# A two-layer GCN and an attention mix on one core: another preparation of degrees, and gather buffers by the chunk

## The chip, the cores and the metric

The kernel runs on one core of a Trainium2 chip. The metric is the device time of one execution in microseconds (us); less is better. PE is TensorE, with PEld its weight loads, DVE is VectorE, ACT is ScalarE, POOL is GpSimd and SP is SyncE, which here only issues DMAs. ACT and POOL issue DMAs too.

## The reference

There are N = 12,500 nodes with D = 256 features and E = 200,000 edges, whose `dst` is sorted. Cut to what matters:

```python
def _gcn_conv(x, W, b, src, dst, n):
    h = x @ W
    ones = jnp.ones(src.shape[0], dtype=x.dtype)
    deg = jax.ops.segment_sum(ones, dst, num_segments=n)
    dinv = jnp.where(deg > 0, jax.lax.rsqrt(deg), 0.0)
    norm = dinv[src] * dinv[dst]
    msgs = h[src] * norm[:, None]
    out = jax.ops.segment_sum(msgs, dst, num_segments=n)
    return out + b

# with self loops appended to src and dst
h = jnp.maximum(_layernorm(x, axis=-1), 0.0)
h = h @ W_pre + b_pre
h = relu(_gcn_conv(h, W1, b1, src, dst, n))
h = relu(_gcn_conv(h, W2, b2, src, dst, n))
x = x + (h @ W_post + b_post)
# a second layer on x: layer norm, relu, x @ weight in 4 heads of 64, a softmax over heads
# of leaky_relu(alpha_l + alpha_r) for the first n edges, a mix of the heads, added to x
```

## The kernel before

The edges are cut into chunks of 14 tiles of 128 edges (`J` = 14, `CE` = 1792): `NCH` = 112 chunks. The nodes form `NT` = 98 tiles of 128, handled in `NG` = 14 groups of `G` = 7. The kernel has four stages.

**Preparation (0 to 161.8 us).** `load_edges` (L536, L538, on SP) brings `dst` and `src` into SBUF as one row per chunk: 111 whole rows in one DMA and the short last one in another. POOL fetches `a_raw`, the first `dst` of every tile, with 30 small DMAs (L561 to L572). `load_x` (L585, on SP) brings node groups into 11 `fxt` buffers. POOL writes constants: `sel`, `iota_r`, `iota_a`, `slide`, `zeros`. DVE casts the list (`fdst_f`, L621) and forms `near` (`dst` less a multiple of 16 per tile) and `to_f` (`dst` less the chunk's first); PE turns these and `src` (`turned`), which gives `near_t`, `to_t` and the gather indices `src_t`.

The degrees are a histogram by products, in four parts of 28 chunks (`NPT`, `CP`). `count_block` compares `near_t` with `iota_r` on DVE (`hot_r`, L699) for four of a chunk's tile positions at a time and sums over edges on PE (`tiles`). `place` adds each part's tiles into the long count: ACT copies `tiles_b`, DVE makes `hot_n` (L722) from the tiles' first ends `a_bf`, PE multiplies (`count`, L728), ACT copies (`counted`), and PE spreads the counts over partitions (`fdegs`, L747). Between blocks, `stats(s)` takes the layer norm's mean and variance of group s (L754, L756). `norms(k)` (L763 on) makes 1/sqrt(degree) and the scales of part k's node tiles, then scales each of its groups (`relu(x * sc + nb)` on ACT at L782; in the last part every second tile on DVE at L778 and L780), writes it to `ftable1` with dinv in a further column (SP, L784), and issues the load of a later group into the freed buffer. `w_of` gives the node tiles that each part completes.

After that come checks of each chunk's range (`lo`, `hi`, `keeps`; they set `bad_row`, by which a general path would be run), the offset of each chunk's window (`offs`), the base of each chunk spread over partitions (`wide`, `base_b`), and the weights of the later products: `fwb`, `fwo` and `fwg`, whose last columns are DVE products with the attention vectors (`far`, `fprod`, L885, L886).

**Pass 1 (161.8 to 2140.4 us) and pass 2 (2140.4 to 4138.2 us).** `convolve` runs over all tiles of all chunks. For each tile POOL gathers 128 rows of the table by an indirect DMA into one of 64 `fgot` buffers (L1043), and PE multiplies them with a one-hot matrix of the destinations (`fhot`, made by DVE for a whole chunk at its predecessor's third tile) and accumulates a chunk in `facc` (L1048). At a chunk's end `close` copies the sums by ACT and puts later steps on a list ordered by tile number: 8 tiles on, PE turns the sums (`fturn`); 13 tiles on, DVE adds them into a sliding window `buf`, and for every node tile that is then complete `finish1` or `finish2` has its steps put on the list, 6, 10 or more tiles on. In pass 1 these are the product with `wf` (`fpo`) and the relu `fo`, which is written to `ftable2`. Pass 2 gathers from `ftable2`; its finish does the second layer's products.

**Mix (4138.2 to 4279.9 us).** POOL gathers the attention terms (`fal`, L1235), and DVE does the softmax and the mix.

Each engine's instructions run in the order in which the program issues them (`manual_schedule`); semaphores for the dependencies between engines are put in by the framework. A tile from a pool with `bufs=n` waits until the n-th tile before it in that name is no longer read.

Of the kernel before, what the change touches and what calls it, by code (L numbers as in the profile page):

```python
# [8 lines left out]
F32 = mybir.dt.float32  # L9
BF16 = mybir.dt.bfloat16  # L10
# [403 lines left out]
def fast_path(  # L414
# [69 lines left out]
    nc.vector.memset(eps, EPS)  # L484

# [7 lines left out]
    row_i = const.tile([P, AC], I32, name="row_i")  # L493
    lane = const.tile([P, 1], F32, name="lane")
    nc.gpsimd.iota(lane, pattern=[[0, 1]], base=0, channel_multiplier=1,
                   allow_small_or_imprecise_dtypes=True)

    def load_w(w, name):
        t = const.tile([P, KC, w.shape[1]], F32, name=name)
        nc.scalar.dma_start(t, w.rearrange("(k p) n -> p k n", p=P))  # L500
        return t
# [5 lines left out]
    with tc.tile_pool(name="fprep", bufs=1) as prep:  # L507
# [3 lines left out]

        LB = 16
        R = 2 * LB
        NL = 2 * LAG + P
        NPT = 4
        CP = NCH // NPT
        L = 7
        Q = CP // L
        I = J * Q
        JB = 4  # L520
        NA = NT * P // LB
        AW = (CP * M + 2 * LAG + P) // LB + 2
        assert NPT * CP == NCH and Q * L == CP and M * CP % LB == 0 and AW % 2 == 0
        a_of = [max(M * CP * k - LAG, 0) // LB for k in range(NPT)]

        w_of = [0] + [((CP * M * (k + 1) - LAG) // P) // G * G for k in range(NPT - 1)] + [NT]
# [4 lines left out]
        def load_edges(e, pad, name):  # L531
            t = prep.tile([NCH, CE], I32, name=name)

            if last < CE:
                nc.vector.memset(t[:, last:], pad)
            nc.sync.dma_start(t[:NCH - 1, :],  # L536
                              e[:(NCH - 1) * CE].rearrange("(c e) -> c e", e=CE))
            nc.sync.dma_start(t[NCH - 1:NCH, :last], e[None, (NCH - 1) * CE:])  # L538
            return t

        dst_r = load_edges(dst, NOWHERE, "fdst_r")
        src_r = load_edges(src, 0, "fsrc_r")
# [8 lines left out]


        a_raw = prep.tile([I, NPT, L], I32, name="a_raw")
        nc.gpsimd.memset(a_raw, NOWHERE)
        for k in range(NPT):
            whole = min(E // CE - k * CP, CP)
            d = dst[k * CP * CE:(k * CP + whole // L * L) * CE].rearrange(
                "(q l j e) -> j q l e", l=L, j=J, e=P)
            a = a_raw[:, k, :].rearrange("(j q) l -> j q l", q=Q)
            for q in range(whole // L):  # L560
                nc.gpsimd.dma_start(a[:, q, :], d[:, q, :, 0])  # L561
            for l in range(whole % L):
                c = k * CP + whole // L * L + l
                nc.gpsimd.dma_start(
                    a[:, whole // L, l:l + 1],
                    dst[c * CE:(c + 1) * CE].rearrange("(j e) -> j e", e=P)[:, 0:1])
        if last < CE:
            j = -(-last // P)
            e = (NCH - 1) * CE
            a = a_raw[:, NPT - 1, L - 1:L].rearrange("(j q) l -> j q l", q=Q)[:, Q - 1]  # L570
            for n in range(j):
                nc.gpsimd.dma_start(a[n:n + 1], dst[None, e + n * P:e + n * P + 1])  # L572
# [19 lines left out]
        for g in range(XB):  # L592
            load_x(g)

# [3 lines left out]
        for r0, base, keep in ((0, 0, [-1, LB - 1]), (R, LB, [1, -LB])):  # L600
# [5 lines left out]
        iota_r = prep.tile([P, R, JB * CP], BF16, name="iota_r")  # L606
        nc.gpsimd.iota(iota_r, pattern=[[1, R], [0, JB * CP]], base=0, channel_multiplier=0,
                       allow_small_or_imprecise_dtypes=True)
        iota_a = prep.tile([I, L, AW], BF16, name="iota_a")
        nc.gpsimd.iota(iota_a, pattern=[[0, L], [1, AW]], base=0, channel_multiplier=0,  # L610
                       allow_small_or_imprecise_dtypes=True)

        slide = prep.tile([P, 2 * I - 1], BF16, name="slide")
        nc.gpsimd.memset(slide, 0.0)
        nc.gpsimd.memset(slide[:, I - 1:I], 1.0)
        zeros = prep.tile([1, 512], BF16, name="zeros")
        nc.gpsimd.memset(zeros, 0.0)


        dst_f = prep.tile([NCH, CE], F32, name="fdst_f")  # L620
        nc.vector.tensor_copy(dst_f, dst_r)  # L621
# [7 lines left out]
                                dst_f.rearrange("c (j e) -> c j e", e=P),  # L629
                                low[:, :, None].to_broadcast([NCH, J, P]), ALU.subtract)  # L630
        base = prep.tile([NCH, 1], F32, name="base")
        nc.vector.tensor_copy(base, dst_f[:, 0:1])
        to_f = dst_f
        nc.vector.tensor_scalar(to_f, dst_f, base, None, op0=ALU.subtract)
        src_f = prep.tile([NCH, CE], F32, name="fsrc_f")
        nc.scalar.activation(src_f, src_r, AF.Copy)
# [8 lines left out]

        with tc.tile_pool(name="wpsum", bufs=2, space=PSUM) as psum:
            wpt = prep.tile([P, KC, D], F32, name="wpt")
            for k in range(KC):
                pt = psum.tile([P, D], F32, name="fw")
                for i in range(KC):  # L650
                    nc.tensor.transpose(pt[:, i * P:(i + 1) * P], wp[:, i, k * P:(k + 1) * P],
                                        ident)
                nc.vector.tensor_copy(wpt[:, k, :], pt)
            for i in range(KC):
# [4 lines left out]
                nc.vector.tensor_copy(wf[:, i, :], pw)  # L659
# [4 lines left out]
            nc.vector.tensor_copy(bb[:1, :], pw[:1, :])  # L664

        with tc.tile_pool(name="fpsum", bufs=2, space=PSUM) as psum, \
# [20 lines left out]
            turned(near, near_t, nc.vector.tensor_copy)  # L687
            turned(to_f, to_t.rearrange("p c j -> p j c"), by_act)
            turned(src_f, src_t.rearrange("p c j -> p j c"), by_act)
            a_int = prep.tile([I, NPT, L], I32, name="a_int")  # L690
            a_bf = prep.tile([I, NPT, L], BF16, name="a_bf")
# [3 lines left out]
            def count_block(k, j0):  # L695
                n = min(JB, J - j0)
                hot = prep.tile([P, R, JB, CP], BF16, name="hot_r", bufs=2)
                near = near_t[:, None, j0:j0 + n, k * CP:(k + 1) * CP]
                nc.vector.tensor_tensor(  # L699
                    hot[:, :, :n, :], near.to_broadcast([P, R, n, CP]),  # L700
                    iota_r[:, :, :n * CP].rearrange("p r (j c) -> p r j c", c=CP), ALU.is_equal)
                if j0 == 0:
                    parts[k] = cpsum.tile([I, R, L], F32, name="tiles", bufs=2)
                for j in range(n):
                    for q in range(Q):
                        i = (j0 + j) * Q + q
                        nc.tensor.matmul(parts[k], slide[:, I - 1 - i:2 * I - 1 - i],
                                         hot[:, :, j, q * L:(q + 1) * L], start=(i == 0),
                                         stop=(i == I - 1))

            def place(k):

                if k == 0:
                    nc.vector.tensor_scalar(a_int, a_raw, LB.bit_length() - 1, None,
                                            op0=ALU.arith_shift_right)
                    for m in range(NPT):
                        nc.vector.tensor_scalar(a_bf[:, m, :], a_int[:, m, :], -float(a_of[m]),
                                                None, op0=ALU.add)
                tiles = prep.tile([I, R, L], BF16, name="tiles_b", bufs=2)
                nc.scalar.activation(tiles, parts[k], AF.Copy)  # L720
                hot = prep.tile([I, L, AW], BF16, name="hot_n", bufs=2)
                nc.vector.tensor_tensor(hot, a_bf[:, k, :, None].to_broadcast([I, L, AW]),  # L722
                                        iota_a, ALU.is_equal)
                a0, a1 = a_of[k], min(a_of[k] + AW, NA)
# [34 lines left out]
            def norms(k):  # L759
# [11 lines left out]
                for g in range(w0 // G, w1 // G):  # L771
                    t = xs[g]
                    nc.vector.tensor_copy(t[:, :, D], dinv[:, g * G:(g + 1) * G])
                    for i in range(G):
                        w = g * G + i
                        h = t[:, i, :D]
                        if k == NPT - 1 and i % 2:
                            nc.vector.tensor_scalar(h, h, sc[:, w:w + 1], nb[:, w:w + 1],  # L778
                                                    op0=ALU.mult, op1=ALU.add)
                            nc.vector.tensor_scalar(h, h, 0.0, None, op0=ALU.max)  # L780
                        else:
                            nc.scalar.activation(h, h, AF.Relu, bias=nb[:, w:w + 1],  # L782
                                                 scale=sc[:, w:w + 1])
                    nc.sync.dma_start(  # L784
                        table1[g * G * P:(g + 1) * G * P, :].rearrange("(c p) d -> p c d", p=P), t)
                    if g + XB < NG:
                        load_x(g + XB)
                nc.vector.reciprocal(dinv2[:, w0:w1], deg[:, w0:w1])

            blocks = [(k, j0) for k in range(NPT) for j0 in range(0, J, JB)]  # L790
            for s, (k, j0) in enumerate(blocks):
                count_block(k, j0)
                if s < NG:
                    stats(s)
# [529 lines left out]
```

## Time and profile before

| | us |
|---|---|
| median of 3 runs | 4279.28 (4278.62 to 4281.58) |
| the profiled execution's own time | 4281.77 |
| its span in the profile | 4279.9 |
| of it: preparation, pass 1, pass 2, mix | 161.8, 1978.6, 1997.8, 141.7 |
| granted TensorE clock, mean | 0.80 |

The profile is of one execution. Its stages are cut at the first gather of each pass and at the first gather of `fal`. A busy share is an average over stages with different limits; idle time ahead of an instruction is put down to the semaphore event that came last before it, and "issue" means that the profile shows nothing that the engine waited for.

### The profile page before, as it was taken

Reading aid. Unit: us, or ns where it says so; the run is one execution under the profiler, and the core shown is the slowest. Engines: PE = TensorE matmul, PEld = TensorE weight load, DVE = VectorE, ACT = ScalarE, POOL = GpSimd, SP = SyncE. Lnnn points to the kernel's source line nnn. Section 1 sums busy time; section 2 is a strip of 40 time slices with the busy share of each in tenths; the row PEclk is TensorE's granted clock in tenths of the full one; section 3 lists DMA queues with packets and bytes.
Section 4 is the critical chain, followed back from the end, with each engine's and each line's share of the span. In section 5 each row is a group of like instructions: output and inputs, shape, how many; then the busy total and the mean of one; then the engine's idle time right before and its main releaser. Section 6 shows DMA issues by size and latency. Waiting matters only on the chain. (4 is left out here: it accounts for less than half of the span.)

```text
span 4279.9 us, 35030 instructions
## 1 busy us (share of the span) xinstructions
PE 3309.1 (77%) x10832; PEld 2027.9 (47%) x10832; DVE 1116.9 (26%) x2279; ACT 407.6 (10%) x1054; POOL 3115.8 (73%) x3297
## 2 busy tenths in 40 slices
PE   5587887878777888778768778777788778887773
PEld 3344444444444444444345555555555545555552
DVE  7422222222222222222122222222222222222238
ACT  3200000000000000000001111111111111111122
POOL 2377777777777777777677777777777777777766
PEclk7677777777777777877878888988888898888886
DMA  5544444444444444444344444444444444444456
GB/s 181 151 118 119 120 121 119 119 119 121 118 119 119 123 119 119 118 121 119 107 142 134 127 124 126 126 123 124 123 127 123 123 123 127 123 123 124 127 155 188
DMA packets 301080, 543.65 MB, mean 127 GB/s; under 512 B 84053, under 2 KB 199508, under 8 KB 300884
## 3 DMA queue, kind: packets, MB, share of 16 engines
q0 software_dynamic: 154480, 414.28, 37.1%
q1 hardware_dynamic: 114958, 111.19, 8.3%
q10 hardware_dynamic: 31446, 15.83, 1.3%
q8 instruction: 90, 1.47, 0.1%
q14 instruction: 106, 0.87, 0.1%
HBM read 488.01 MB, written 52.93 MB: 126 GB/s over the span
## 5 line engine op out<-in xcount | busy, mean ns | idle before, releaser
L1043 POOL DMA_INDIRECT fgot<-ftable,fsrc_t x3126 | 2982.8, 954 | 1026.7 <-issue 474.2
L1048 PE MATMUL facc<-fgot,fhot 128*128 128x257 f32 (+1 forms) x6252 | 2385.5, 500 | 774.3 <-DMA fgot<-ftable,fsrc_t 738.5
L1048 PEld LDWEIGHTS facc<-fgot,fhot 128*128 128x128 f32 x6252 | 1233.1, 230 | 1784.6 <-DMA fgot<-ftable,fsrc_t 1451.2
L997 DVE TENSOR_TENSOR buf<-buf,fturn 128x256 f32 x224 | 94.5, 422 | 1707.0 <-PE fturn L941 1675.0
L974 DVE TENSOR_TENSOR fhot<-iota_p,to_t 128x1792 f32<-128x1792 f32 x224 | 448.3, 2003 | 0.1
L1129 DVE SCALAR_TENSOR_TENSOR fx<-fpo,fdinv,fxb 128x256 f32<-128x256 f32 x97 | 46.9, 484 | 1311.2 <-PE fpo L1125 1311.2
L981 ACT ACTIVATE fsums<-facc 128x257 f32<-128x257 f32 (+1 forms) x224 | 86.4, 386 | 1352.9 <-PE facc L1048 1352.8
L1077 PE MATMUL fpo<-wf,buf 128*128 128x256 f32 x388 | 162.3, 565 | 0.4 <-DVE buf L997 0.4
L1112 PE MATMUL fpz<-buf,fwb 128*128 128x128 f32 x776 | 147.2, 319 | 0.0
L1077 PEld LDWEIGHTS fpo<-wf,buf 128*128 128x128 f32 x388 | 118.3, 305 | 30.8 <-DVE buf L997 0.7
L1235 POOL DMA_INDIRECT fal<-table_l,fsrc_t x98 | 94.9, 968 | 50.6 <-issue 27.1
L1112 PEld LDWEIGHTS fpz<-buf,fwb 128*128 128x128 f32 x776 | 121.2, 220 | 14.9 <-issue 3.6
L1082 ACT ACTIVATE fo<-fpo,fdinv 128x256 f32<-128x256 f32 x97 | 46.0, 474 | 807.5 <-PE fpo L1078 807.5
L941 PE MATMUL fturn<-fident,self 128*128 128x128 f32 x396 | 89.5, 314 | 34.7 <-DMA self<-ftable 30.0
L1124 PE MATMUL fpo<-fwo,fz 128*128 128x256 f32 x388 | 114.8, 422 | 0.0
L1114 PE MATMUL fpz<-rm,fb2r 1*128 1x128 f32 x388 | 104.3, 352 | 0.0
L941 PE MATMUL fturn<-fident,fsums 128*128 128x128 f32 x448 | 101.7, 315 | 0.5 <-ACT fsums L981 0.5
L1226 PE MATMUL fends<-rows,hot_t 128*128 128x260 f32 x196 | 67.7, 519 | 39.7 <-ACT fxg L1228 39.4
L1013 DVE COPY buf<-buf 128x640 f32<-128x640 f32 x194 | 97.5, 502 | 3.3
L941 PEld LDWEIGHTS fturn<-fident,fsums 128*128 128x128 f32 x448 | 74.3, 166 | 35.9 <-issue 13.1
L1078 PE MATMUL fpo<-bb,fins 2*128 2x256 f32 x194 | 87.3, 537 | 0.0
L941 PEld LDWEIGHTS fturn<-fident,self 128*128 128x128 f32 x396 | 59.9, 167 | 42.9 <-issue 31.6
(198 smaller groups left out, 1602.0 us busy)
## 6 DMA issues: line engine op xcount, KB each, us to landing
fgot<-ftable,fsrc_t POOLq DMA_INDIRECT x3126, 2.8
ftable<-fxt SPq DMA_DIRECT2D x14, 910.0 KB
self<-ftable SPq DMA_DIRECT2D x97, 130.0 KB
ftable<-fo ACTq DMA_DIRECT2D x98, 128.0 KB
kept_x<-fx SPq DMA_DIRECT2D x98, 128.0 KB
fxr<-kept_x SPq DMA_DIRECT2D x14, 896.0 KB
self<-ftable SPq DMA_DIRECT2D x97, 128.0 KB
fxb<-in_x_dram SPq DMA_DIRECT2D x97, 128.0 KB
```

Of the source, the lines that this page charges most:

```text
L941: nc.tensor.transpose(v["pt"][:, i * KC + k, :], rows[:, k * P:(k + 1) * P], ident)
L974: nc.vector.tensor_tensor(h[:, :n, :], iota_p[:, None, :].to_broadcast([P, n, P]), to_t[:, c, :n, None].to_broadcast([P, n, P]), ALU.is_equal)
L997: nc.vector.tensor_add(b, b, v["pt"][:, :KC, :])
L1013: nc.vector.tensor_copy(nxt[:, :, :BW - P], buf[:, :, P:])
L1043: nc.gpsimd.indirect_dma_start(out=got, out_offset=None, in_=table[:], in_offset=bass.IndirectOffsetOnAxis(ap=src_t[:, c, j:j + 1], axis=0))
L1048: nc.tensor.matmul(acc, hots[c][:, j, :], got[:, :width], start=(j == 0), stop=(j == nj[c] - 1))
L1077: nc.tensor.matmul(po, buf[:, k, :P], wf[:, k, :], start=(k == 0), stop=False)
L1078: nc.tensor.matmul(po, fs, bb, start=False, stop=True)
L1112: nc.tensor.matmul(pz[:, m, :], wb[:, k, m * P:(m + 1) * P], buf[:, k, :P], start=(k == 0), stop=False)
L1114: nc.tensor.matmul(pz[:, m, :], b2r[:, m * P:(m + 1) * P], v["rm"], start=False, stop=True)
L1124: nc.tensor.matmul(po, v["z"][:, m, :], wo[:, m, :], start=(m == 0), stop=False)
L1235: nc.gpsimd.indirect_dma_start(out=al[:, i, :], out_offset=None, in_=table_l[:], in_offset=bass.IndirectOffsetOnAxis(ap=src_t[:, c, j:j + ...
```

## The change

1. `load_edges` issues the 111 whole rows as two DMAs of 96 and 15 rows. The `src` list is issued behind the first two loads of x.
2. The 30 DMAs of `a_raw` and the shift and subtraction on it go. In their place a 0/1 tensor `perm`, made on POOL, is reduced in two ways (`by_kq`, `by_kl`); POOL multiplies `low` with the one (`low_q`), PE multiplies that with the other, and ACT scales the product into `a_bf`.
3. POOL's constants are made in another order: `zeros`, `slide` and `iota_r` first, `sel` last.
4. DVE works on the integer list itself (no `fdst_f`). The copies of `wpt`, `wf`, `bb` and `near_t` move from DVE to ACT. An activation `warm` at the start loads the Sqrt table. `src` is cast and turned after the second block.
5. The degrees are counted in five parts of 28, 28, 28, 21 and 7 chunks (`c_of`), with as many tile positions per block as fit (`JB`). `stats(0)` runs before the first block, and then each block is followed by the next group's `stats`. `norms` only lists its groups in `to_scale`; one of them is scaled after each block, and those left over at the end. The copy of dinv into its column moves from DVE to POOL. `dinv2` is taken once, at the end.
6. The small operations for `offs` move up, most of them to POOL. The check of the chunks' ranges is now made from `to_t` (`check_chunks`), and the loads of the late weights and the products with `far` become `load_late`; both are called in pass 1 after the first `fo`.
7. `fgot` is allocated once per chunk as a tile of 14 gathers, with 4 buffers, in place of 64 buffers of one gather.

The diff, cut to its core:

```diff
-        NPT = 4
-        CP = NCH // NPT
+        c_of = [0, 28, 56, 84, 105, NCH]
+        NPT = len(c_of) - 1
+        CP = [c_of[k + 1] - c_of[k] for k in range(NPT)]
...
-        JB = 4
+        BLOCK = 4 * max(CP)
+        JB = [min(BLOCK // n, J) for n in CP]
...
-            nc.sync.dma_start(t[:NCH - 1, :],
-                              e[:(NCH - 1) * CE].rearrange("(c e) -> c e", e=CE))
+            some = (NCH - 1) // 16 * 16
+            for c0, c1 in ((0, some), (some, NCH - 1)):
+                nc.sync.dma_start(t[c0:c1, :],
+                                  e[c0 * CE:c1 * CE].rearrange("(c e) -> c e", e=CE))
...
-        src_r = load_edges(src, 0, "fsrc_r")
...
-        a_raw = prep.tile([I, NPT, L], I32, name="a_raw")
-        nc.gpsimd.memset(a_raw, NOWHERE)
...
         for g in range(XB):
             load_x(g)
+            if g == 1:
+                src_r = load_edges(src, 0, "fsrc_r")
...
+        perm = prep.tile([NCH, NPT, max(Q), L], F32, name="perm")
+        nc.gpsimd.memset(perm, 0.0)
+        for k in range(NPT):
+            p = perm[:, k, :Q[k], :]
+            nc.gpsimd.affine_select(out=p, in_=p, compare_op=ALU.not_equal, fill=1.0,
+                                    base=-c_of[k], pattern=[[-L, Q[k]], [-1, L]],
+                                    channel_multiplier=1)
...
-        dst_f = prep.tile([NCH, CE], F32, name="fdst_f")
-        nc.vector.tensor_copy(dst_f, dst_r)
...
+        for k, q in enumerate(Q):
+            nc.gpsimd.tensor_mul(low_q[k], low[:, :, None].to_broadcast([NCH, J, q]),
+                                 by_kq[:, k, None, :q].to_broadcast([NCH, J, q]))
...
+        nc.gpsimd.tensor_copy(mean_i, mean)
+        nc.vector.tensor_scalar(mean_i, mean_i, ~(P - 1), None, op0=ALU.bitwise_and)
...
-            turned(near, near_t, nc.vector.tensor_copy)
+            turned(near, near_t, by_act)
+            a_bf = prep.tile([I, NPT, L], BF16, name="a_bf")
+            pa = psum.tile([I, NPT, L], F32, name="ft")
+            for k, q in enumerate(Q):
+                nc.tensor.matmul(pa[:J * q, k, :], low_q[k].rearrange("c j q -> c (j q)"),
+                                 by_kl[:, k, :], start=True, stop=True)
+                nc.scalar.activation(a_bf[:J * q, k, :], pa[:J * q, k, :], AF.Copy,
+                                     scale=1.0 / LB, bias=-float(a_of[k]))
...
+            stats(0)
+            blocks = [(k, j0) for k in range(NPT) for j0 in range(0, J, JB[k])]
             for s, (k, j0) in enumerate(blocks):
                 count_block(k, j0)
-                if s < NG:
-                    stats(s)
+                if s + 1 < NG:
+                    stats(s + 1)
...
+                if s == 1:
+                    turn_src()
+                if to_scale:
+                    scale(k == NPT - 1)
             norms(NPT - 1)
+            while to_scale:
+                scale(True)
+            nc.vector.reciprocal(dinv2, deg)
...
-            got = ep.tile([P, stride], F32, name="fgot", bufs=ahead)
+            if j == 0:
+                gots = ep.tile([P, J, stride], F32, name="fgot", bufs=ahead)
+            got = gots[:, j, :]
...
             nc.scalar.dma_start(table2[w * P:(w + 1) * P, :], o)
+            if w == 0:
+                load_late(work)
+                check_chunks(work, psum)
...
-        convolve(ep, table1, D1, D + 1, 64, True, psum, lambda w: prepare1(work, w),
+        convolve(ep, table1, D1, D + 1, 4, True, psum, lambda w: prepare1(work, w),
...
-        convolve(ep, table2, D, D, 64, False, psum, lambda w: prepare2(work, w),
+        convolve(ep, table2, D, D, 4, False, psum, lambda w: prepare2(work, w),
```

## The prediction, made before the changed kernel ran

> **What bounds the kernel now.** I read the page's totals first, then the table of busy time by stage, then what GpSimd (POOL) waits for.
>
> ```profile
> span 4279.9 us, 35030 instructions
> PE 3309.1 (77%) x10832; PEld 2027.9 (47%) x10832; DVE 1116.9 (26%) x2279; ACT 407.6 (10%) x1054; POOL 3115.8 (73%) x3297
> ...
> L1043 POOL DMA_INDIRECT fgot<-ftable,fsrc_t x3126 | 2982.8, 954 | 1026.7 <-issue 474.2
> ```
>
> ```profile
> 0.00:161.80 161.80, 75.23 (x395) 58.81 (x395) 107.72 (x343) 61.09 (x129) 31.27 (x66) 0.69 0.59 182
> 161.80:2140.40 1978.60, 1585.26 (x4343) 863.83 (x4341) 421.31 (x831) 89.85 (x210) 1491.09 (x1564) 0.76 0.44 119
> 2140.40:4138.20 1997.80, 1583.25 (x5906) 1056.10 (x5907) 482.34 (x919) 218.49 (x604) 1498.63 (x1570) 0.85 0.47 125
> 4138.20:4279.90 141.70, 65.31 (x192) 49.19 (x190) 105.56 (x186) 38.16 (x112) 94.86 (x98) 0.72 0.69 210
> ```
>
> The columns are length, then busy us (instructions) of PE, PEld, DVE, ACT and POOL, then clock, DMA share and GB/s. Both passes are rows of gathers on POOL: 1,563 of them at 1.251 us each (0.947 busy, 0.305 before the next) make 1,955 of pass 1's 1,979 us. PE is busy 80% of a pass, but is only a follower: a gather's matmul ends 3.4 to 9.2 us after that gather starts, 28.0 once, as pass 2 begins.
>
> ```profile
> POOL fgot L1043 <- issue: 474.2, 1519, 11.6
> POOL fgot L1043 <- PE facc L1048: 382.3, 1255, 0.3
> POOL fgot L1043 <- DVE sbuf L957: 63.2, 1, 63.2
> ```
>
> 382.3 us is put down to PE, yet no wait among the 1,255 is over 0.3 us, the gap that gathers with no such wait have too. The first 64 gathers take fresh buffers and never wait for PE. Here are 63 of them beside 63 later ones, which all do:
>
> ```profile
> L1043 POOL DMA_INDIRECT fgot<-ftable,fsrc_t x63 | 60.0, 952 | 82.1 <-DVE sbuf L957 63.2 <-issue 18.9
> ...
> L1043 POOL DMA_INDIRECT fgot<-ftable,fsrc_t x63 | 60.4, 959 | 19.2 <-issue 11.3 <-PE facc L1048 6.1 <-PE fsum L943 0.6
> ```
>
> 18.9 us of gaps without, 19.2 with. So the passes go by POOL's own rate, and what can move is the 161.8 us before the first gather. There VectorE (DVE) is the chain:
>
> ```profile
> 17.25 1.09 DVE L621 CAST fdst_f<-fdst_r 112x1792 f32<-112x1792 int32 x1 [14.81 <-DMA fdst_r<-in_dst_dram]
> 37.67 1.37 DVE L682 CAST near_t<-ft 128x448 bf16<-128x448 f32 x2 [9.74 <-PE ft L680]
> 40.23 2.02 DVE L699 TENSOR_TENSOR hot_r<-near_t,iota_r 128x3584 bf16<-128x3584 bf16 x1
> 134.24 0.19 DVE L763 TENSOR_SCALAR fdeg<-fdegs 128x28 f32<-128x28 f32 x1 [15.03 <-PE fdegs L747]
> 143.81 1.96 DVE L804 TENSOR_REDUCE flo<-fdst_f 112x1 f32<-112x1792 f32 x1
> 157.51 0.42 DVE L885 TENSOR_TENSOR fprod<-fwg,far 128x256 f32<-128x256 f32 x1 [3.14 <-DMA self<-ftable]
> 161.81 1.04 POOL L1043 DMA_INDIRECT fgot<-ftable,fsrc_t  x1 [63.23 <-DVE sbuf L957]
> ```
>
> It waits for the edge list until 17.25; for POOL's constants (PE's first matmul needs `zeros`, ready at 35.6 behind 18 us of `a_raw` DMAs) until 37.67; counts from 40.23 with hardly a break to 119.2; waits 15 us for the last fourth of the degrees; scales four groups (8.2 us); checks chunks from 143.81 to 152.57; and makes `fwg` last. The last four writes of `ftable1`, which share the queues with weight loads, end at about 152.
>
> **Part 1, a start 21 us earlier.** The trace shows the 111 rows of `dst` moving three at a time, 37 rows per DMA engine, 3.8 to 16.5. As 96, 15 and 1 rows they can use more engines: six rows each of about 0.3 to 0.55 us. I take a landing at 8. Bounds: 6.5 (uncontended) and 17.25 (unspread, as now). [...]
>
> DVE drops the 1.09 cast; low, `near`, base and `to_f` (0.17+0.17+2.02+0.15+1.15) with two reductions end about 12.8. It then meets `mean_i`, which waits for POOL. POOL's list without `a_raw`: 1.7 + memsets 0.70 + zeros 0.51 + slide 0.31 + `iota_r` 3.29 = 6.5; perm (a memset, five selects of 0.1 to 0.3) 7.4; `iota_a` 1.54, 8.9; sel 5.6, 14.5; five `low_q` products, which no row shows: between 0.1 (small memset) and 1.08 (select on 1,024 elements), I take 0.2, nearest in size, 15.5; mean 16.1. Then `stats(0)`, 2.8 us, to 19.0, and the first `hot_r` at 19.0 in place of 40.23. Its other input, `near_t`, moves to ACT: the table load of 1.28 us, now at the head of ACT's queue, delays the weight loads' issue by as much, the weight chain (PE products, copies of about 0.4 on ACT) ends near 13.4, and four copies of 0.87 end by 17.6, inside that wait. The product for the tiles' ends (five PE-ACT rounds of about 0.8) and the `to_t` copies end at 25.3 on ACT; nothing needs the ends before the first `hot_n`. On SP the `src` load now stands behind x 0 and x 1: at 2.6 to 3.3 us a load, as the x loads take now, it lands near 17, x 2 near 20 and x 10 near 45, each ahead of its `stats` (one per 4.6 us); `src` is first read after block 1, about 28.
>
> **Part 2, counting to the last degrees.** DVE's sum stays: `hot_r` 27 us, 13 remaining `stats` at 2.77 = 36, `hot_n` 6.8, four `norms` about 4.9: 74.6 us, so 19.0 → 93.6. What follows is the short last part (7 chunks) on PE and ACT: third part's degrees (count 1.4, copy 0.7, eight matmuls 3.6) at 98.9, last block 101.1, its count, copy and degrees 107.0. Its `norms` end at 108.6, against 135.4 now. Interleaved scaling of g0 to g8, one group a block, lies on ACT under the blocks; their writes and the loads of x 11 to 13 on SP run one a block, 4.6 us apart, each 2.8 us of transfer. If that cover fails, the later `stats` are late by one transfer. The copy of `dinv` moves to POOL (0.17 on DVE), which has nothing else then but memsets waiting for those writes.
>
> **Part 3, the last groups and the exit.** Now four groups are scaled last, then five, 2.03 each: 108.6 + 10.2 = 118.7. The first is ready to write at 110.6 and five writes at 2.8 us (8.4 us for three in the trace where no weight shared the queue) drain at about 125.2, landing at 126. DVE's remainder (dinv2, `offs`, degrees, `wide`, `root_t`) ends at 122.6, under the drain. Chunk checks (8.8) and `fwg` (3.25 plus 3.14 waiting) have left this path, and weight loads too. With the 1 us that POOL takes over semaphores now, the first gather is at 127: 161.8 − 127 = **35 us earlier**.
>
> **Part 4, inside pass 1.** `load_late` and `check_chunks` follow the first `fo`, at about gather 50: some eight issues on ACT (0.5 each), a stall of 6 to 8 us for the second `far` buffer, 15 us of DVE work and waits, three transposes on PE. Behind DVE's wait stand the next `fhot` (2.0 us) and so PE's matmuls; POOL feels it only when a buffer is not free. Cost 0. Without that cover, up to 15 us.
>
> **Part 5, one tile per chunk.** 2,998 waits of POOL for PE become 216, each chunk's first gather waiting for the matmul 43 gathers before it, 43 × 1.251 = 53.8 us of slack against 9.2 (28.0 once). By the two rows of 63 gathers the dropped waits are worth 0.3 us in 63, or nothing; bounds 0 to 2,782 × 5 ns = 14 us of gain. I take 0. About 104 gathers, some 47 in each pass, last 1.0 to 1.7 us and cost 23 us in all; they come at the same places of a chunk whether the gather carries no, one or two waits, so I leave them. The stretch between the passes (11.6) and the ending stay.
>
> **Sum.** 4281.77 (profiled execution, 1.87 outside its span) − 35 = 4246.8. It stands 2.5 above the median, so 4279.3 − 35 = **4244.3**, say 4245.
>
> **Rivals.** *Less from preparation* (0.16): `dst` unspread, so the change does not do what it says (−5.5, since POOL's list hides the rest), `low_q` at its upper end (−4.4), a drain at 3.5 us a write (−3.5). Together the gain is 21.6: 4258. For: ACT carries more, and no row shows most of POOL's small products. Against: the waits of 14.81 and 9.74 have visible causes that go.
>
> *Faster passes* (0.05): if part of the 0.305 gap is the handling of a wait, 20 ns each is 56 us, 4189. The two rows of 63 speak against. [...]
>
> *Slower* (0.06): releasing by the chunk makes POOL wait. Place: each chunk's first gather; it decides once PE runs over 53.8 us behind. At 0.3 us for each of 216 waits it costs 65, net +30: 4309; the break-even is 0.16 us a wait. Against: PE has 20% of a pass free, so even the stall of part 4 is worked off within some four chunks. For: a buffer comes free only when its whole chunk is multiplied, and part 4 lands on PE while the queue is full.
>
> *Preparation gains under 9* (0.03): a stall in the x loads behind writes on SP, 4272 to 4279.
>
> **Chances and range.** Forecast 0.70, a gain of 25 to 42 (25: the bounds of part 1 and a drain that is 3 us longer; 42: the drain keeps pace, so that the last write ends 3.8 after 118.7, and POOL's list is 3 us shorter). The measurement tells about 0.2%, 8.6 us, from no change. Faster: 0.70 + 0.16 + 0.05 = 0.91; same 0.03; slower 0.06. The range takes in the forecast's bounds (4237 to 4254), most of the lesser gain (to 4262), and 5 us at the lower end for part 5's bound in the gaps: 4232 to 4262.
>
> **What would show it.** First `hot_r` at about 19; no wait over 2 us on DVE before the third part's degrees; the last degrees at 107; first gather at 127; gathers at 1.251, gap 0.305, and no POOL wait for PE above 0.3. Wrong if the gap shrinks in every gather, or first gathers of chunks wait, or the first gather comes after 140.

## The result, and the profile after

The changed kernel takes 4245.18 us (median of 4, 4243.32 to 4246.28) against 4279.75 for the kernel before: a ratio of 0.9918, 95% interval 0.9901 to 0.9936. That is 34.6 us less; 35 were forecast. Its page and its table by stage (the columns are those explained in the prediction):

```profile
span 4243.1 us, 32312 instructions
PE 3275.7 (77%) x10867; PEld 2000.0 (47%) x10867; DVE 1116.3 (26%) x2257; ACT 409.1 (10%) x1066; POOL 3102.3 (73%) x3304
...
L1077 POOL DMA_INDIRECT fgot<-ftable,fsrc_t x3126 | 2978.4, 953 | 985.1 <-issue 954.1
```

```profile
0.00:126.50 126.50, 74.47 (x421) 58.82 (x421) 98.24 (x298) 62.77 (x141) 22.62 (x74) 0.68 0.71 222
126.50:2106.20 1979.70, 1568.72 (x4350) 852.22 (x4350) 430.29 (x854) 89.83 (x210) 1489.19 (x1563) 0.77 0.43 119
2106.20:4101.30 1995.10, 1566.38 (x5906) 1039.26 (x5907) 482.50 (x919) 218.52 (x604) 1495.76 (x1570) 0.86 0.47 125
4101.30:4243.10 141.80, 66.14 (x192) 49.72 (x190) 105.32 (x186) 38.03 (x112) 94.75 (x98) 0.72 0.69 209
```

Preparation is 35.3 us shorter, and the other three stages moved by +1.1, −2.7 and +0.1 us. The page's instruction count fell by 2,718 (POOL alone has 2,783 semaphore waits fewer), and the gathers did not notice: 953 ns each, 954 before. What POOL waits for changed its name and not its amount:

```profile
POOL fgot L1077 <- issue: 954.1, 3024, 18.8
POOL fgot L1077 <- PE facc L1082: 25.0, 82, 0.3
```

The 382.3 us that were put down to PE are now "issue"; the gap of 0.3 us stays in front of every gather. The steps of preparation, on DVE, POOL and ACT:

```profile
9.13 0.82 DVE L614 TENSOR_SCALAR low_i<-fdst_r 112x14 int32<-112x14 int32 x1 [6.69 <-DMA fdst_r<-in_dst_dram]
10.19 2.81 DVE L619 TENSOR_TENSOR near_f<-fdst_r,low 112x1792 f32<-112x1792 int32 x1
18.94 0.15 DVE L651 TENSOR_SCALAR mean_i<-mean_i 112x1 int32<-112x1 int32 x1 [4.03 <-POOL mean_i L650]
21.78 2.00 DVE L734 TENSOR_TENSOR hot_r<-near_t,iota_r 128x3584 bf16<-128x3584 bf16 x1
99.15 0.18 DVE L794 TENSOR_SCALAR fdeg<-fdegs 128x21 f32<-128x21 f32 x1 [2.37 <-PE fdegs L778]
103.36 0.29 DVE L798 RECIPROCAL fdinv<-froot 128x21 f32<-128x21 f32 x1 [3.83 <-ACT froot L796]
106.75 0.17 DVE L794 TENSOR_SCALAR fdeg<-fdegs 128x7 f32<-128x7 f32 x1 [0.72 <-PE fdegs L778]
```

```profile
11.19 2.77 POOL L609 TENSOR_SCALAR_AFFINE_SELECT sel<-sel 32x1024 f32<-32x1024 f32 x1
14.00 1.85 POOL L607 TENSOR_SCALAR_AFFINE_SELECT sel<-sel 32x1024 f32<-32x1024 f32 x1
15.92 1.08 POOL L609 TENSOR_SCALAR_AFFINE_SELECT sel<-sel 32x1024 f32<-32x1024 f32 x1
...
126.47 1.24 POOL L1077 DMA_INDIRECT fgot<-ftable,fsrc_t  x1 [18.75 <-issue]
```

DVE has the list at 9.1, counting starts at 21.8, the wait of 15 us for the last degrees is now 0.7 behind one of 3.83, the last group is scaled at 117.5, the packets of its write end at 124.7, and the first gather is at 126.5.

### The profile page after: what moved, and what is told of

It is laid out like the page before. It is cut to its first block, busy times and chain, and to the rows that moved or that the text cites. A ratio compares the mean times of both kernels' runs of the same rounds, so it can differ in the third digit from the quotient of the medians.

```text
span 4243.1 us, 32312 instructions
## 1 busy us (share of the span) xinstructions
PE 3275.7 (77%) x10867; PEld 2000.0 (47%) x10867; DVE 1116.3 (26%) x2257; ACT 409.1 (10%) x1066; POOL 3102.3 (73%) x3304
## 5 line engine op out<-in xcount | busy, mean ns | idle before, releaser
L1082 PEld LDWEIGHTS facc<-fgot,fhot 128*128 128x128 f32 x6252 | 1215.9, 228 | 1798.4 <-DMA fgot<-ftable,fsrc_t 1462.9
L1263 PE MATMUL fends<-rows,hot_t 128*128 128x260 f32 x196 | 68.6, 526 | 38.9 <-ACT fxg L1265 38.7
L972 PEld LDWEIGHTS fturn<-fident,fsums 128*128 128x128 f32 x448 | 72.8, 163 | 34.4 <-issue 11.5
```

Source lines behind the costliest of these rows:

```text
L972: nc.tensor.transpose(v["pt"][:, i * KC + k, :], rows[:, k * P:(k + 1) * P], ident)
L1082: nc.tensor.matmul(acc, hots[c][:, j, :], got[:, :width], start=(j == 0), stop=(j == nj[c] - 1))
```

## The experiments

The first gather's time is the sharper meter for what changes in preparation: it is read from the trace of one run, while single runs of the passes differ by some 5 us. It has a spread of its own: six traces with the changed kernel's preparation (the changed kernel, E2, E3, E4, E9 and E12) have it at 125.5, 126.3, 126.4, 126.5, 126.6 and 127.9, so one trace does not tell a difference of less than some 2.5 us. Four runs (E1 to E4) were on a chip that granted TensorE a clock of 0.71 to 0.75 where all others granted 0.79 to 0.82; the kernel before took 4966 there. They are told last, with E9 and E12, which repeat E2 and E3 at 0.81.

### E5: the edge lists as 111 rows and 1 row again

```diff
-            for c0, c1 in ((0, some), (some, NCH - 1)):
+            for c0, c1 in ((0, NCH - 1),):
```

> The changed kernel with the edge lists loaded as 111 rows and 1 row again. Theory by the changed trace: dst lands near 16.5 and not 9.1; near, base and to_f end near 22, and the mean by POOL comes before that; stats(0) to 25 and the first hot_r at 25 in place of 21.8; the first gather 3 us later, 129 to 130. The prediction priced it at 5.5. Rival (the whole delay of the list, 7.4 us, is passed on): first gather at 134.

Measured: 4257.17, first gather at 139.87, 13.4 us later than in the changed kernel. The first `hot_r` is only 5.4 later, at 27.2. DVE's timeline of this run shows the rest:

```profile
18.86 0.17 DVE L613 TENSOR_SCALAR low_i<-fdst_r 112x14 int32<-112x14 int32 x1 [16.42 <-DMA fdst_r<-in_dst_dram]
...
41.82 2.38 DVE L784 BATCH_NORM_STATS2 fstats<-fxt 128x6 f32<-128x256 f32 x7 [7.94 <-DMA fxt<-in_x_dram]
```

The third group of x (x 2) is late, and the trace shows two things ahead of it. SP stands until the first list has landed, and so issues `src` only at 18.86 (8.38 in the changed kernel) and x 2 at 19.54 (9.68):

```profile
SPq L541 <- DMA fdst_r<-in_dst_dram: 7.4, 1, 7.4
```

Then the `src` rows, three at a time again, move from 22.7 to 38.7. That shares of x 2 wait behind them is an inference: the profile does not say which DMA engine moved a packet. So without the splitting the first gather is 13.4 us later, 5.4 of it by the first `hot_r` and 7.9 by the wait for x 2. Both theories were low, and the prediction's price of 5.5 had left out `src`.

### E6: the chunk checks ahead of pass 1 again

```diff
+    with tc.tile_pool(name="fwork0", bufs=1) as work, \
+            tc.tile_pool(name="psum0", bufs=1, space=PSUM) as psum:
+        check_chunks(work, psum)
...
-                check_chunks(work, psum)
```

> The changed kernel with the chunk checks made ahead of pass 1 again (in their new form). Theory (they stand behind 121.1 on DVE and cost some 7 us there, of which the drain of the last writes hides 4 to 5): first gather at 129, 2 to 4 us later. Rival (no cover): 7 to 9 us later, 133.5 to 135.5.

Measured: 4255.04, first gather at 133.07, 6.6 later: between the theory and the rival, and close to the rival.

```profile
125.59 1.78 DVE L882 TENSOR_REDUCE far<-to_t 128x112 f32<-128x1568 f32 x1 [4.43 <-DMA ftable<-fxt]
...
131.85 0.14 DVE L902 TENSOR_SCALAR bad<-n_kept 1x1 int32<-1x1 f32 x1
```

The checks take 6.4 us from 125.59. They get no cover from the last writes, since they wait for them: the tile that they fill takes memory freed by preparation. This run therefore prices the checks without cover; with memory of their own they could have lain under the drain, which was not tried.

### E7: the late loads and products ahead of pass 1 again

```diff
+        load_late(work)
...
-                load_late(work)
```

> The changed kernel with the late weight loads and the products with the attention vectors made ahead of pass 1 again. Theory: the weights (0.8 MB) share the queues with the last writes and put their end off by 2.5 us; DVE's products (3.3 us) wait for two loads of the attention vectors, one after the other: first gather 4 to 8 us later, 130 to 134. PE's lag of 20.7 near gather 50 goes. Rival (the products hide under the drain): not over 2.5 us later, 129.

Measured: 4261.76, first gather at 139.58, 13.1 later; both theories were low.

```profile
132.34 0.42 DVE L916 TENSOR_TENSOR fprod<-fwg,far 128x256 f32<-128x256 f32 x1 [10.84 <-DMA self<-ftable]
...
136.71 0.42 DVE L916 TENSOR_TENSOR fprod<-fwg,far 128x256 f32<-128x256 f32 x1 [2.58 <-DMA far<-in_L_gnn_attn_l_dram]
```

The end of the last writes moves from 124.7 to 127.3, with the weights' packets beside them. ACT issues the first `far` load only at 128.16, behind those writes, and the second at 133.71, behind the first's products. ACT waits there for the landing of those writes, so this run, too, carries a wait for memory that comes of its placement. Of the 13.1, some 2.5, the later end of the writes, and the 6.2 from 132.34 to the end of the last product (2.58 of them waiting) belong to the work itself.

### E8: four parts of 28 chunks again

```diff
-        c_of = [0, 28, 56, 84, 105, NCH]
+        c_of = [0, 28, 56, 84, NCH]
```

> The changed kernel with the degrees in four parts of 28 chunks again (the rest of the change stays, five groups are still scaled last). Theory by the changed trace (the fifth part spares the last chain only a count of 1.4 - 0.6 us and copies, and costs a chain of its own on ACT, with 3.8 us of waiting): last degrees at 104 to 108, first gather at 125 to 128. Rival (the small last part is what removes the 15 us wait for the last degrees): last degrees at 112 or later, first gather at 132 or later.

Measured: last degrees at 104.00, as the theory had it; first gather at 123.85, 2.6 us *earlier* than in the changed kernel and earlier than expected (the one run took 4246.70; its pass 2 was 4.8 longer). The rival falls: without the small last part the wait of 15 us does not come back, and DVE waits 3.33 us for the last degrees. Where the 15 us came from is seen on ACT. In the kernel before, the copy of the last part's tiles stands behind 28 scalings; in E8 ACT is free and waits for PE:

```profile
114.26 13.87 ACT L782 ACTIVATE fxt<-fxt,fnb,fsc 128x256 f32<-128x256 f32 x28 [0.89 <-ACT froot L765]
128.03 0.33 ACT L720 ACTIVATE tiles_b<-tiles 56x224 bf16<-56x224 f32 x1
```

```profile
98.34 0.35 ACT L750 ACTIVATE tiles_b<-tiles 56x224 bf16<-56x224 f32 x1 [4.11 <-PE tiles L742]
```

So the small last part is not what removed the wait. By these rows it is the spreading of the scaling over the blocks, which takes the 28 tiles from this place; no run undoes the spreading alone. That the fifth part costs time is less sure than that it brings none. E8's first gather lies 1.6 us below the lowest of the six traces, and it is one trace. Besides, with four parts the code gives DVE every second tile of the groups scaled between the blocks of the last 28 chunks, which also relieves ACT. The fifth part does add a chain of its own: the 3.83 us on DVE in the after profile are ACT scaling g7 and copying the fifth part's tiles before it comes to the fourth part's `froot`.

### E10: sel behind the mean

The block that makes `sel` (a memset, four selects) moves behind POOL's small operations.

> The changed kernel with the POOL work on sel (memset and four selects) moved behind the small operations on the mean. In the changed kernel DVE waits 4.0 us for the mean that stands behind sel on POOL, and two of the selects last 2.8 and 1.9 us beside DVE's near_f, which itself lasts 2.8. Theory (both engines slow each other, and the wait is on the path): near_f at 2.0, mean_i without a wait, first hot_r at 17 to 18 in place of 21.8, last degrees 4 us earlier and the first gather at 122 to 123. Rival (the rest of preparation is set by PE or by the writes and loads one after another): first hot_r earlier, first gather at 125 to 126.5.

Measured: first `hot_r` at 17.30, degrees at 102.7 in place of 106.75, first gather at 122.33, 4.1 earlier (the one run took 4245.95; its passes took 4.9 more).

```profile
9.43 2.02 DVE L609 TENSOR_TENSOR near_f<-fdst_r,low 112x1792 f32<-112x1792 int32 x1
...
14.46 0.15 DVE L641 TENSOR_SCALAR mean_i<-mean_i 112x1 int32<-112x1 int32 x1 [1.24 <-POOL mean_i L640]
```

`near_f` is back at 2.02 with the same integer input and with POOL idle beside it (9.02 to 11.74): it was POOL's work beside it that made it 2.81. The wait for the mean is 1.24 us and not nought as expected. Of the 4.5 us gained at the start of counting, 4.1 are left at the last degrees and at the first gather.

### E11: three edits for a faster kernel

E10's move, E8's four parts, and a second group scaled after the last block:

```diff
-                if to_scale:
+                for _ in range(min(len(to_scale), 2 if s + 1 == len(blocks) else 1)):
                     scale(k == NPT - 1)
```

> The changed kernel with sel moved as in the run before, four parts of 28 chunks, and two groups scaled after the last block in place of one, so that four groups remain at the end and the writes of ftable1 start earlier. Theory: 4 us for sel, 2.6 for the parts, 3 for the write that is taken out of the last drain: first gather at 116 to 118, time 8 to 10 us below the changed kernel, 4235 to 4237 where the kernel before takes 4280. Rival (the second scaled group delays the last degrees on DVE or ACT by as much): 4238 to 4242.

Measured: 4235.51 (4233.49 to 4236.24), ratio to the kernel before 0.9891, interval 0.9875 to 0.9908; E9 on the same chip has the changed kernel's preparation and took 4245.73. First gather at 117.99. Time and first gather are where the theory had them. The writes now run without a break from 99.6 to 116.4, so the drain ends 8.3 us earlier than in the changed kernel.

### E1 and E2: the release by the chunk, done alone and undone alone

E1 puts item 7 into the kernel before, E2 takes it out of the changed one:

```diff
-            got = ep.tile([P, stride], F32, name="fgot", bufs=ahead)
+            if j == 0:
+                gots = ep.tile([P, J, stride], F32, name="fgot", bufs=ahead)
+            got = gots[:, j, :]
```

> The kernel before with one edit: gather buffers by the chunk (4 tiles of 14) in place of 64 single ones, so that POOL waits for PE 216 times and not 2,998. Theory (the passes go by POOL's own rate, gap 0.305 with or without a wait): the same time within 4 us, gather pitch 1.251. Rival (each wait is part of the gap, 20 ns): 56 us faster, 4224. Rival (release by the chunk makes POOL wait): first gathers of chunks come late by more than 0.3 us.

> The changed kernel with single gather buffers (64) put back. Theory (all of the gain is ahead of the first gather): 4245, first gather at 126.5, pitch 1.251. Rival (part of the gain is in the passes): slower than the changed kernel by that part, up to 35 us.

Measured on the chip of the lower clock: before 4966.13, E1 4983.74 (ratio 1.0039, 1.0025 to 1.0052), E2 4935.48 (0.9935, 0.9917 to 0.9953). Both theories missed. First gathers are at 161.5 and 125.5, as elsewhere; each pass is 290 to 360 us longer, and the mix some 50. E1's POOL timeline and its PE timeline inside pass 1:

```profile
1035.50 0.95 POOL L1046 DMA_INDIRECT fgot<-ftable,fsrc_t  x1 [0.30 <-issue]
1041.74 0.94 POOL L1046 DMA_INDIRECT fgot<-ftable,fsrc_t  x1 [5.29 <-remote]
```

```profile
1008.72 4.93 PE L1051 MATMUL facc<-fgot,fhot 128*128 128x257 f32 x22
...
1027.00 0.59 PE L1051 MATMUL facc<-fgot,fhot 128*128 128x257 f32 x1 [0.84 <-issue]
1029.11 0.59 PE L1051 MATMUL facc<-fgot,fhot 128*128 128x257 f32 x1 [1.52 <-issue]
1031.90 0.59 PE L1051 MATMUL facc<-fgot,fhot 128*128 128x257 f32 x1 [2.21 <-issue]
```

The gathers themselves still go at 1.25, and then POOL stands for 5.3 us. PE runs in bursts, and between them starts a matmul only every 1.4 to 2.8 us, with data long landed and nothing to wait for that the profile shows. In E1 its lag (from a gather's start to the end of its matmul) is some 48 us in pass 1 and 59 in pass 2, where it is 4 on the other chips; that is about the depth of the buffers. So E1's second rival, the prediction's "slower", has come true on this chip: PE is the bound, and POOL waits for it, 639 us in all at 149 gathers of E1, the pass boundary among them (609 us at 336 gathers of E2, which may go on as soon as one buffer is free). The coarser release costs E1 0.39%, 18 us. The changed kernel itself was not run on this chip.

That the lower clock is the cause is not shown. A matmul into `facc` takes 380 ns at full clock and 635 at half on both chips, and PE is busy for only 57% of E1's pass 1. What differs is that stretches at half clock last 27 us at the median of E1's pass 1 and 7 in the changed kernel's, and that 565 of the 645 us of PE's unexplained gaps of over 0.6 us there lie in stretches at half clock; the changed kernel's pass 1 has no such gap at either clock. Whether PE stands because of the clock or the clock is low because PE stands, no run here tells.

### E9: E2 once more

> The changed kernel with single gather buffers (64), once more, since the first time TensorE's granted clock was 0.72 and PE fell as far behind as the buffers allow. Theory (where the clock is 0.8, PE keeps up and the kind of release is worth nothing): 4242 to 4248, first gather at 125.5 to 126.5, pitch 1.251. Rival (the release by the chunk brings or costs something there too): outside 4240 to 4250.

Measured at 0.81: 4245.73 (4241.65 to 4250.80), ratio 0.9916, interval 0.9900 to 0.9933, beside 0.9918 for the changed kernel. The time and the pitch are as the theory had them; the first gather is not, at 127.91 (the reason stands under part 2 below). Apart from the gap between the passes no gather comes more than 0.35 us after the one before it ends, in either. 2,782 waits more or fewer are worth nothing here.

### E3, E12 and E4: less slack

The changed kernel with 2 chunk buffers (E3, E12) and with 1 (E4):

```diff
-        convolve(ep, table1, D1, D + 1, 4, True, psum, lambda w: prepare1(work, w),
+        convolve(ep, table1, D1, D + 1, 2, True, psum, lambda w: prepare1(work, w),
```

> The changed kernel with 2 chunk buffers in place of 4: a chunk's first gather waits for the matmul 15 gathers before it, 18.8 us of slack. In the changed kernel's trace PE lags its gathers by 4 us, 20.7 after the late loads near gather 50, and 27.6 as pass 2 begins. Theory (a wait costs POOL only what the lag exceeds the slack by): up to 2 us near gather 50 and up to 9 at the start of pass 2, so 4245 to 4256. Rival (a wait by the chunk has a price of its own, 0.3 us each): 65 us more, 4310.

> The changed kernel with 2 chunk buffers, once more, for a granted clock of 0.8 (the first time it was 0.71). Theory (the release costs only what PE's lag exceeds the 18.8 us of slack by; the changed kernel's trace shows 20.7 near gather 50, 27.6 as pass 2 begins, and 8 elsewhere): 0 to 11 us more, 4245 to 4256, and POOL waits for PE near gather 50 and at the start of pass 2 alone. Rival (a price at each chunk): 4270 or more. Where the clock should be 0.71 again: 4950 to 4980.

> The changed kernel with 1 chunk buffer: a chunk's first gather waits for the matmul of the gather just before it. Theory (POOL then waits for the lag less one pitch): PE's lag at a chunk's last gather is 3.4 us at least, 3.9 on average in pass 1 and 5.1 in pass 2, so 2.15 to 3.9 us at each of 222 chunk starts: 480 to 720 us more, 4720 to 4965. Rival (other work, such as the sums and windows, has to be waited for too): over 4965.

E12, at 0.81, took 4256.88 beside 4289.97 for the kernel before on the same chip: ratio 0.9924 (0.9907 to 0.9940), the changed kernel's within its interval. It is just above its theory's range, on a chip where the kernel before is slower too, and the expected waits did not come: POOL waits for PE nowhere, though the lag reaches 20.5 near gather 51 and 28.6 at the start of pass 2: only a chunk's *last* matmul counts, and at those its lag is at most 18.2, just inside the slack of 18.8. (That chip's gathers last 949 ns, 946 in the changed kernel's trace, and 3 ns 3,126 times are 9 us, in both kernels.) At 0.71, E3 took 4963.96, ratio 0.9990 (0.9968 to 1.0012), with 685 us of waiting. E4, also there, took 4990.97 (one run), above the range of its theory: 203 of its 227 late gathers start 2.8 to 3.5 us after the one before ends, and the waits sum to 716, the upper end of what was expected at the usual clock. With POOL waiting at each chunk, PE's lag is back to 4 and its granted clock is 0.75. What one buffer costs at 0.8 stays untried.

## Why the prediction was right

**The place was right.** It said that POOL paces the passes at 1.251 and that only the time before the first gather could move. The passes moved by −1.6 us together; the first gather by −35.3 (forecast 127, measured 126.47). E9, with 64 single buffers and the new preparation, has the whole gain.

**Part 1 was too good by 2.8 us.** The rows of the list landed at 8.0 as forecast, but DVE started on them at 9.1 (before: 16.3 and 17.25). That 96 rows would use more engines, six rows on each, was the author's assumption: no trace of before shows it, and the profile does not say which DMA engine moved a packet, so 37 rows per engine is an inference too. The packets of `dst` show, in the kernel before, three rows in flight for 11.5 of the 12.5 us from 3.8 to 16.3, and in the changed kernel up to 18, 16 for the longest share (1.4 of 4.3 us), from 3.7 to 8.0; a row's packet took 0.27 to 0.60 us before and 0.42 at the median after. Why 111 rows go three at a time, no run tells. POOL's list was taken as undisturbed: `sel` was priced at 5.6 us and took 8.0 with two selects of 2.77 and 1.85, `near_f` 2.81 for 2.02; so the mean came at 18.9 and not 16.1. Five `low_q` products took 1.14, near the 1.0 taken, and 2.00 in E10. Two of the prediction's signs failed here: the first `hot_r` was at 21.8 and not about 19, and DVE had a wait of over 2 us, 4.03 for the mean. The second sign did not fit part 1 to begin with, which has DVE standing from 12.8 to 16.1.

**Part 2 was too bad by as much.** DVE's sum held: from 21.8 to the end of `hot_n` 75.0 us (74.6 forecast; one of the four `norms` came only after that, and a wait of 1.05 for PE came in). The chain on PE and ACT behind it was over-priced: last degrees 10.0 us after that (13.4 forecast), so that they came at 106.75 for 107.0. The step is the fourth part's degrees (the prediction counts from nought and calls it the third), 2.4 us after `hot_n` where 5.3 were forecast. The 16 matmuls that make a part's degrees were priced at 3.6 us; they take that where the record shows half clock, and 1.96 where it shows full clock. Here are the fourth and the fifth part's in the changed kernel, then the fourth's in E9:

```profile
97.16 1.96 PE L778 MATMUL fdegs<-counted,sel 64*128 64x21 f32 x16 [0.70 <-ACT counted L709]
103.13 3.58 PE L778 MATMUL fdegs<-counted,sel 64*128 64x7 f32 x16 [0.52 <-ACT counted L709]
```

```profile
97.63 3.60 PE L778 MATMUL fdegs<-counted,sel 64*128 64x21 f32 x16 [0.70 <-ACT counted L709]
```

E2 had both at full clock: last degrees at 105.9, first gather at 125.5. E9, with the same end of `hot_n`, had them at 108.3 and 127.9. That the two errors of 2.8 us cancel is luck, and so is the agreement to 0.5 us at the first gather: another execution moves it by more. The credit given to the short last part was wrong (E8: it brings nothing, and may cost up to 2.6).

**Part 3 held.** Scaling ended at 117.5 (118.7), the writes at 124.7 (125.2), DVE's remainder at 121.1 (122.6): the drain is what the first gather waits for, and E11 shows it from the other side. That checks and late loads would cost where they stood is shown by E6 and E7, with waits for memory in their price.

**Part 4 held.** PE stands 13.4 us for the checks near gather 51 and its lag goes to 20.7; it is back at 3.5 by gather 78, and no gather was late. The stall for the second `far` buffer was 2.9 us of waiting on DVE, where 6 to 8 were forecast.

**Part 5 held where the granted clock was 0.8** (E9, E12), and with it the rival of faster passes falls. The 104 long gathers that it counted include five of the mix; the passes have 99, 88 in the changed kernel and 108 in E9, so they vary by themselves. No run shows the 20 ns a wait that the rival of faster passes assumed: the gap is 0.305 us with 2,998 waits (E9) and with 216 (the changed kernel). The rival "slower" was dismissed by PE's free fifth of a pass. That holds on the chips at 0.80 and fails on the one at 0.71, where PE was busy for still less of pass 1 (57%) and yet fell behind: a low busy share was no proof that PE could catch up. E1 measured the price, 18 us and not the rival's 65.

**The range of cases was right but for one price.** If the rows had not spread, the gain would have been 21 to 23 (E5, by its first gather and by its one run's time) and not 29.5.

**What stays read from the traces alone.** No run puts back the 30 DMAs of `a_raw` (item 2), the copies on DVE (item 4) or the scaling at the part's end (item 5). Nor are the 13.4, 6.6 and 13.1 us of E5, E6 and E7 shares of the 35.3: each of these runs has waits that the kernel before did not have.

## What to carry to other kernels

When one engine paces the long stages, read the time ahead of its first instruction as a chain of its own, and follow it to the last write that the next stage reads; there, work that was saved for the end (the scaling and its writes) stood in the way, and making the last part small brought nothing. Undo parts one by one: the part with a good argument (a small last part) brought nothing, and undoing the one that looked like a detail of a DMA (96 rows) cost 13.4 us, more than half of it in the wait for a later load behind a second one. Repeat a trace before you read 2 us from it: the same preparation ended 2.4 us apart. Here a release in larger lots was free where the follower kept up (the changed kernel at a ratio of 0.9918, E9 at 0.9916) and cost 18 us on the chip where it did not (E1).

## What the runs showed of the hardware that was not expected

- A wait for PE, whether 2,998 or 216 of them, does not lengthen POOL's gap between gathers: 0.305 us in each case (E9 and the changed kernel).
- In the changed kernel POOL and DVE slowed each other. `near_f` started while a select ran and took 2.81 us, 2.02 in E10 with POOL idle beside it; the next select started while `near_f` ran and took 2.77, where the four selects of the kernel before took 1.08 each. The select that ran as `near_f` started took 1.13. By what they slow each other, no run here tells.
- The same 16 small matmuls take 1.96 us at full granted clock and 3.6 at half, and which of the two they meet differs between executions of the same preparation (E2, E9 and the changed kernel).
- On the one chip with a granted clock of 0.71 to 0.75 the same kernels took 16% longer, and in E1 PE was idle for 40% of the span while it was the bound, starting a matmul every 1.4 to 2.8 us between bursts. What holds it between them, no view of the profile shows; it stays open.
